# Blockwise VectorE transposes of x in the projections of a graph attention kernel

## The chip, the cores and the metric

The kernel runs on one core of one Trainium2 chip. The metric is the device time of one execution in microseconds (us): the median of several runs. A separate profiled execution gives the spans, waits and durations that this text quotes.

## What is computed

x has 3327 rows of 512 features in float32, adj is a 3327 x 3327 matrix of zeros and ones. A block of two attention layers is followed by a binarised linear layer. Cut to what matters:

```python
def gat_layer(x, W, adj):                 # twice, with W_stack[0] and W_stack[1]
    Wh, Ws = split(x @ W, 2, axis=-1)     # W is 512 x 1024
    a = softmax((Wh @ Ws.T), axis=-1) * adj
    return leaky_relu(a @ Wh + x, 0.01)

y = layernorm(x + gat_layer(gat_layer(x, W0, adj), W1, adj))
xw = maximum(sign(y), 0) @ sign(weight).T
out = layernorm(y + relu(adj @ xw))
```

## The kernel before

**Stages.** For each of the two layers l the kernel runs `project(l)` and then `attention(l)`; a last stage, `finale`, multiplies adj with the binarised layer's output. The change lies in `project`.

**Tiles.** A row tile is 128 rows of x (26 of them, t = 0 to 25; the last has 127 rows). A chunk c is four row tiles (7 chunks, 0 to 6; the last has two tiles). The 512 features are cut into four blocks k of 128 (`KD` = 4). TensorE contracts over partitions, so the projections need x with features on partitions: `xT[c]` is a tile of 128 partitions x 4 blocks k x 512 columns, a column being a row of x. There are two such buffers.

**From x to xT.** `load_x(c)` issues one DMA per row tile on SP (rows on partitions, 2 KB each; the last tile in two pieces of 112 and 15 rows). For layer 0 the source is x, for layer 1 it is x1_d, which attention of layer 0 writes. `transpose_x(c, k, lane)` makes one block k of xT: one TensorE transpose (L263) for each row tile of the chunk into a PSUM bank, and then one copy of 128x512 from PSUM into xT: by ScalarE (L268), or for chunk 0 by ScalarE and VectorE in turn (L121, L123 in `copy_out`). A chunk is so four such calls. For the last chunk GpSimd sets the one column without a row to zero (L273).

**W.** `load_x(0)`, the loads of W's left half into `wa` (L279) and right half (`load_w`, L207) and `load_x(1)` stand at the head of SP's queue in layer 0. W's rows are on partitions, in four blocks of 128 consecutive rows. The scores are computed as x M x^T with M = the Wh-half of W times the transposed Ws-half; `transpose_w` (L213) and `product_m` (L235) make M. For layer 1 this happens inside attention of layer 0.

**The projections.** Products are done by a seven-product scheme (Strassen-Winograd form): `seven` writes out the seven products with their copies and additions, `left_sums` (L180 to L183) and `right_sums` (L186 to L189) make the sums of operands on VectorE. For each pair of row tiles `keys(c, a)` makes the left sums of xT and stores xT and the sums to xs_d through GpSimd's queue (L325 to L327), and `project_values(c, a)` does the seven products with W (L338) and stores right sums of the result to ws_d. For each chunk `queries(c)` makes the right sums of xT (names xt) and does twice seven products with M and its sums msum (L394), and stores to gs_d.

**Order.** The main loop of `project` works on chunk c while it prepares chunk c + 1:

```python
turns = [lambda k=k: transpose_x(c + 1, k, tr_lane) for k in range(KD)]
pairs_of[c + 1] = project_values(c + 1, 0, acc_lane)
turns += [pairs_of[c + 1].pop(0), lambda: prepare(c + 1)]
```

`turns` are the four transposing steps, the left sums of the next chunk's first pair and the right sums of the next chunk. `weave` puts them in between the products of chunk c, evenly spread. x of chunk c + 2 is loaded at the start of the turn of chunk c. Each engine works off its own list in order and waits where an operand is not there yet. The row tiles, sums and many other tiles share a ring of buffers of 2 KB a partition (`slot`); a load waits until its buffer is free. In layer 1 the loads of the binarised layer's weights (L462) stand on SP among the loads of x, and their two operations per block (neg_w, L464, and bw, L466) among VectorE's work.

Of the kernel before, what the change touches and what calls it, by code (L numbers as in the profile page):

```python
# [9 lines left out]
F32 = mybir.dt.float32  # L10
# [9 lines left out]
P = 128  # L20
CT = 4
CW = CT * P
HW = CW // 2
NEG_SLOPE = 0.01
EPS = 1e-5
# [4 lines left out]
def kernel(  # L30
# [8 lines left out]
    nc = tc.nc  # L39
    N, D = x.shape  # L40
    L = w_stack.shape[0]
    KD = D // P
# [6 lines left out]
    def rows(t):  # L49
        return min(P, N - t * P)  # L50

    def tiles_of(c):
        return range(c * CT, min(NT, (c + 1) * CT))

    def halves_of(c):
        return [g for g in (2 * c, 2 * c + 1) if g < NQ]
# [5 lines left out]
    def half_cols(g):  # L62

        return g * HW, min(HW, N - g * HW)

# [11 lines left out]
    def slot(shape, dtype, name):  # L77
        return ring.tile(shape, dtype, tag="s", bufs=SBUFS, name=name)

    ident = keep.tile([P, P], F32, name="ident")  # L80
# [27 lines left out]
    ws_d = [tc.dram_tile([NQ, P, 4, HD], F32, name=f"ws_d{l}") for l in range(L)]  # L108
    gs_d = [tc.dram_tile([NC, P, 7, 2, HW], F32, name=f"gs_d{l}") for l in range(L)]

    def load_rows(eng, dst, src, r):

        cut = r - r % 16
        if cut:
            eng.dma_start(out=dst[:cut], in_=src[:cut])
        if cut < r:
            eng.dma_start(out=dst[cut:r], in_=src[cut:r])

    def copy_out(n, dst, src):
        if n % 2:  # L120
            nc.scalar.copy(dst, src)  # L121
        else:
            nc.vector.tensor_copy(dst, src)  # L123
# [20 lines left out]
    def seven(lane, name, multiply, c11, c12, c21, c22):  # L144
# [5 lines left out]
        def product(i, b, start):  # L150
            if start:
                bank[b] = pool.tile([P, HW], F32, tag=tag, name=f"p{b}_{name}")
            multiply(i, bank[b], start)

        def copied(i, b):
            if not held:
                two = slot([P, 2, HW], F32, f"h0_{name}"), slot([P, 2, HW], F32, f"h1_{name}")
                held.update(zip(("p1", "p5", "u2", "u3"), (t[:, e] for t in two for e in (0, 1))))
# [32 lines left out]
    def weave(*lists):  # L191

        at = [
            ((i + 0.5) / len(part), n, do)
            for n, part in enumerate(lists) for i, do in enumerate(part)
        ]
        for _, _, do in sorted(at, key=lambda e: e[:2]):
            do()

    ch_lane, acc_lane, tr_lane = (ps_ch, "ch"), (ps_acc, "acc"), (ps_tr, "tr")  # L200
    w_rows, wT, m_of, wsum_of = {}, {}, {}, {}

    def load_w(l, h):

        for k in range(KD):
            w_rows[l, h, k] = slot([P, D], F32, f"w{h}_{l}_{k}")
            nc.sync.dma_start(out=w_rows[l, h, k], in_=w_stack[l, ts(k, P), ts(h, D)])  # L207

    def transpose_w(l, h, k, lane):
        pool, tag = lane  # L210
# [32 lines left out]
    def project(l, pre):  # L243

        src = x if l == 0 else x1_d
        xTs, rows_of = {}, {}

        def load_x(c):
            rows_of[c] = []
            for t in tiles_of(c):  # L250
                xt = slot([P, D], F32, f"xr_{l}_{t}")
                load_rows(nc.sync, xt, src[t * P : t * P + rows(t), :], rows(t))
                rows_of[c].append(xt)

        def transpose_x(c, k, lane):
            if k == 0:
                xTs[c] = pre.tile([P, KD, CW], F32, tag="xT", bufs=2, name=f"xT_{l}_{c}")
            pool, tag = lane
            pt = pool.tile([P, CW], F32, tag=tag, name=f"pxt_{l}_{c}_{k}")
            w = 0  # L260
            for a, t in enumerate(tiles_of(c)):
                r = rows(t)
                nc.tensor.transpose(  # L263
                    pt[:, w : w + r], rows_of[c][a][:r, ts(k, P)], ident[:r, :r]
                )
                w += r
            if c:
                nc.scalar.copy(xTs[c][:, k, :w], pt[:, :w])  # L268
            else:
                copy_out(k, xTs[c][:, k, :w], pt[:, :w])  # L270
            n = len(tiles_of(c)) * P
            if w < n:
                nc.gpsimd.memset(xTs[c][:, k, w:n], 0.0)  # L273


        load_x(0)
        wa = pre.tile([P, KD, D], F32, tag="wa", bufs=1, name=f"wa_{l}")
        for k in range(KD):
            nc.sync.dma_start(out=wa[:, k], in_=w_stack[l, ts(k, P), :D])  # L279
        if l == 0:  # L280
            load_w(l, 1)
            for k in range(KD):
                w_rows[l, 0, k] = wa[:, k]
        load_x(1)
        for k in range(KD):
            transpose_x(0, k, acc_lane)
        if l == 0:
            for h in range(2):
                for k in range(KD):
# [5 lines left out]
        lo, hi = wa[:, 0:2], wa[:, 2:4]  # L295
# [34 lines left out]
        def project_values(c, a, lane):  # L330
            q = c * CT // 2 + a
            of = {}
            b12 = slot([P, HD], F32, f"wb12_{l}_{q}")
            b11, b21, b22 = (wh[q][:, i] for i in range(3))

            def multiply(i, bank, start):
                for k in range(2):
                    nc.tensor.matmul(  # L338
                        bank, of[LEFT[i]][:, k], wr[RIGHT[i]][:, k],
                        start=(start and k == 0), stop=(k == 1), skip_group_check=True,  # L340
                    )

            def done():
                t12 = slot([P, 2, HD], F32, f"t12_{l}_{q}")
                t34 = slot([P, 2, HD], F32, f"t34_{l}_{q}")
                right_sums(b11, b12, b21, b22, t12[:, 0], t12[:, 1], t34[:, 0], t34[:, 1])
                nc.gpsimd.dma_start(out=ws_d[l][q][:, 0:2], in_=t12)
                nc.gpsimd.dma_start(out=ws_d[l][q][:, 2:4], in_=t34)

            return (  # L350
                [lambda: of.update(keys(c, a))]
                + seven(lane, f"wh_{l}_{q}", multiply, b11, b12, b21, b22) + [done]
            )

        def queries(c, lanes):
# [3 lines left out]
            gs = {  # L359
                i: slot([P, 2, HW], F32, f"gsp_{l}_{c}_{i}")  # L360
                for i in (range(7) if len(halves_of(c)) == 2 else (B11, B21))
# [6 lines left out]
            if len(halves_of(c)) == 1:  # L368
                def one(e):
                    pg = ps_ch.tile([P, HW], F32, tag="ch", name=f"pg_{l}_{c}_{e}")  # L370
                    for k in range(KD):
                        nc.tensor.matmul(
                            pg, m[:, k, ts(e, P)], xT[:, k, :HW],
                            start=(k == 0), stop=(k == KD - 1),
                        )
                    copy_out(e, gs[B11 if e < 2 else B21][:, e % 2], pg)
# [44 lines left out]
        def prepare(c):  # L421
            start, *chains[c] = queries(c, (ch_lane, ch_lane if c else acc_lane))
            if start:
                start()
# [10 lines left out]
        for c in range(NC):  # L435
            turns = []
            if c + 1 < NC:
                turns = [lambda k=k: transpose_x(c + 1, k, tr_lane) for k in range(KD)]
                pairs_of[c + 1] = project_values(c + 1, 0, acc_lane)
                turns += [pairs_of[c + 1].pop(0), lambda: prepare(c + 1)]  # L440
            turns = rest + turns
            rest = [chains[c][1].pop()] if chains[c][1] else []
            if c + 2 < NC:
                load_x(c + 2)
            if c == 0:
                weave(*chains[c], turns)
            else:
                one, two = chains[c]
                pairs = pairs_of[c]
                for a in range(1, len(tiles_of(c)) // 2):  # L450
                    pairs += project_values(c, a, acc_lane)
                rest.append(pairs.pop())
                weave(one + two, pairs, turns)
# [15 lines left out]
    def attention(l, att):  # L469
# [116 lines left out]
        def column_max(c):  # L586
# [22 lines left out]
            def back():  # L609
                pb = ps_tr.tile([P, CW], F32, tag="tr", name=f"poff_{l}_{c}")  # L610
                for a in range(n):
                    nc.tensor.transpose(pb[:, ts(a, P)], rep[a], ident)
                for i, g in enumerate(halves_of(c)):
                    off[g] = att.tile([P, 1, HW], F32, tag=f"off{i}", bufs=1,
                                      name=f"off_{l}_{g}")
                    nc.vector.tensor_copy(off[g][:, 0], pb[:, ts(i, HW)])
# [336 lines left out]
    xw, xw_tiles, xt, ah, po = {}, [], {}, {}, {}  # L953
# [51 lines left out]
    def finale(att):  # L1005
# [78 lines left out]
        for g in range(NQ):  # L1084
# [30 lines left out]
            for _, do in sorted(work, key=lambda e: e[0]):  # L1115
                do()
        inexact = nc.values_load(flag_i[0:1, 0:1], min_val=0, max_val=2 * CW)
        with tc.If(inexact < 1) as cmp:
# [70 lines left out]
```

## Time and profile before

| | us |
|---|---|
| median of 3 runs | 2652.82 (2652.31 to 2653.39) |
| the profiled execution: its time | 2652.55 |
| the profiled execution: its span | 2650.7 |
| ScalarE copies of xT (L268), 48 | 26.5 busy |
| TensorE waiting for VectorE or ScalarE in the projection of layer 1 | 1.4 |
| TensorE waiting for the first loads of x in layer 0 | 5.6 |

The span is the time from the first to the last instruction of the profiled execution; 1.85 us lie around it. "Busy" is the time in which an engine had an instruction running; matmuls overlap one another, so that the distance between the starts of two of them and not their duration tells what one costs. PE is TensorE, PEld its loads of the stationary operand, DVE VectorE, ACT ScalarE, POOL GpSimd, and SP issues most of the loads. The projection of layer 0 takes the first 190 us or so, that of layer 1 lies between about 1257 and 1430 us. The chain of waits that ended last consists of TensorE's matmuls of the final product and, at the very end, of the additions and the normalisation of the last rows.

### The profile page before, as it was taken

To read this page: it belongs to the slowest core of one execution; us is meant where nothing else is said; L and a number is where in the kernel's file an instruction comes from. 1 tells how busy PE (TensorE), PEld (TensorE's weight loads), DVE (VectorE), ACT (ScalarE), POOL (GpSimd) and SP (SyncE) were. 2 spreads that over 40 slices of the span, in tenths; PEclk is the share of its full clock that TensorE was granted. 3 is DMA by queue.
4 is the path that set the end of the run, shared out by engine and by line. 5 is a ranking of instruction groups with operands and counts; after the bars stand their busy time and mean duration, and the time that the engine had idled before them with its cause. 6 is when DMAs were issued, how large, how long until landed. Compare 5 with 4: busy or idle time off the path is not lost. (4 is left out here: it accounts for less than half of the span.)

```text
span 2650.7 us, 40451 instructions
## 1 busy us (share of the span) xinstructions
PE 2614.6 (99%) x12839; PEld 2271.0 (86%) x12864; DVE 2046.3 (77%) x4211; ACT 812.1 (31%) x2000; POOL 1091.3 (41%) x2029
## 2 busy tenths in 40 slices
PE   9999999999999999999999999999999999999998
PEld 7888888888888888887888888888888888888787
DVE  5554888899888896666754589988899888767976
ACT  3333332333333332221333333333333333222143
POOL 2550343444444444546552044444444444455510
PEclk9999999999999999999999999999999999999999
DMA  5754777777777776776865677777777777677875
GB/s 205 272 193 157 260 239 251 253 266 252 259 244 244 267 248 222 235 245 230 294 219 180 210 231 272 241 257 260 233 270 247 252 255 236 228 260 260 278 245 168
DMA packets 285186, 638.63 MB, mean 241 GB/s; under 512 B 32141, under 2 KB 146671, under 8 KB 283430
## 3 DMA queue, kind: packets, MB, share of 16 engines
q1 hardware_dynamic: 249206, 529.52, 60.4%
q0 software_dynamic: 35760, 106.45, 10.8%
q8 instruction: 105, 1.72, 0.3%
q14 instruction: 115, 0.94, 0.1%
HBM read 528.91 MB, written 106.93 MB: 240 GB/s over the span
## 5 line engine op out<-in xcount | busy, mean ns | idle before, releaser
L500 PE MATMUL pZ<-gs,xs 128*128 128x256 f32 x2496 | 636.2, 379 | 1.7 <-ACT u L517 1.7
L699 POOL TENSOR_TENSOR as<-s 128x128 f32<-128x128 f32 x338 | 163.4, 484 | 1037.0 <-DVE s L661 691.9
L500 PEld LDWEIGHTS pZ<-gs,xs 128*128 128x128 f32 x2496 | 473.3, 190 | 67.8 <-ACT u L517 3.6
L726 PE MATMUL acc<-ws,s 128*128 128x256 f32 x1352 | 402.6, 379 | 0.0
L726 PE MATMUL acc<-wh,s 128*128 128x256 f32 x1352 | 355.9, 379 | 0.0
L726 PE MATMUL acc<-ws,as 128*128 128x256 f32 x1352 | 349.7, 380 | 1.8 <-POOL as L701 1.2
L648 ACT ACTIVATE s<-s 128x512 f32<-128x512 f32 x338 | 213.3, 631 | 377.7 <-DVE s L645 377.1
L500 PE MATMUL pY<-gs,xs 128*128 128x256 f32 x1248 | 320.7, 379 | 2.2 <-ACT p L517 2.2
L726 PEld LDWEIGHTS acc<-ws,as 128*128 128x128 f32 x1352 | 255.2, 190 | 42.3 <-issue 5.8
L726 PEld LDWEIGHTS acc<-wh,s 128*128 128x128 f32 x1352 | 257.3, 190 | 35.2
L726 PEld LDWEIGHTS acc<-ws,s 128*128 128x128 f32 x1352 | 256.2, 190 | 34.4
L570 DVE TENSOR_TENSOR top<-top,s 128x512 f32<-128x512 f32 x312 | 225.4, 735 | 69.0 <-ACT s L557 48.5
L500 PEld LDWEIGHTS pY<-gs,xs 128*128 128x128 f32 x1248 | 236.7, 190 | 36.0 <-ACT p L517 3.8
L645 DVE TENSOR_TENSOR s<-s,off 128x512 f32<-128x512 f32 x338 | 249.2, 737 | 0.1
L661 DVE TENSOR_TENSOR s<-s,adj 128x512 f32<-128x512 f32 x338 | 236.8, 701 | 9.4 <-DMA adj<-in_adjT_dram 1.0
L656 DVE TENSOR_TENSOR total<-total,s 128x512 f32<-128x512 f32 x312 | 231.8, 743 | 0.0
L517 ACT COPY u<-pZ 128x256 f32<-128x256 f32 x312 | 115.8, 371 | 345.5 <-PE pZ L500 344.9
L701 POOL TENSOR_TENSOR as<-s 128x128 f32<-128x128 f32 x338 | 204.7, 606 | 26.5
L726 PE MATMUL acc<-wh,as 128*128 128x256 f32 x676 | 203.0, 382 | 0.0
L700 POOL TENSOR_TENSOR s<-s 128x128 f32<-128x128 f32 x338 | 183.3, 542 | 27.6
L702 POOL TENSOR_TENSOR as<-s,as 128x128 f32<-128x128 f32 x338 | 180.7, 535 | 26.5
L542 DVE TENSOR_TENSOR s<-p,u 128x256 f32<-128x256 f32 x156 | 66.8, 428 | 151.7 <-ACT u L517 151.7
(206 smaller groups left out, 3883.9 us busy)
## 6 DMA issues: line engine op xcount, KB each, us to landing
ws<-ws_d SPq DMA_DIRECT2D x338, 512.0 KB, 3.8
xs<-xs_d SPq DMA_DIRECT2D x182, 512.0 KB, 5.8
adj<-in_adjT_dram SPq DMA_DIRECT2D x324, 256.0 KB, 4.2
xs<-xs_d SPq DMA_DIRECT2D x156, 384.0 KB, 6.5
gs_d<-gsp POOLq DMA_DIRECT2D x88, 256.0 KB, 2.8
gs<-gs_d SPq DMA_DIRECT2D x12, 1792.0 KB, 10.9
adj_d<-ab POOLq DMA_DIRECT2D x169, 112.0 KB, 3.8
ahl<-adj_d SPq DMA_DIRECT2D x78, 224.0 KB, 4.7
```

What stands on the lines that cost most here:

```text
L500: nc.tensor.matmul(ch[bank], xs[c, q, a][:, k], gs[c][:, b, k], start=(start and k == 0), stop=(k == 1), skip_group_check=True,)
L517: nc.scalar.copy(ch[name], ch[bank])
L570: nc.vector.tensor_tensor(top[i], top[i], t, ALU.max)
L645: nc.vector.tensor_tensor(s, s, off[g].to_broadcast([P, 2, HW]), ALU.subtract)
L648: nc.scalar.activation(sc[g, q], sc[g, q], AF.Exp)
L656: nc.vector.tensor_tensor(total[g], total[g], sc[g, q], ALU.add)
L661: nc.vector.tensor_tensor(s, s, adj[g, q], ALU.mult)
L699: nc.gpsimd.tensor_tensor(s3, a11, a21, ALU.subtract)
L700: nc.gpsimd.tensor_tensor(a21, a21, a22, ALU.add)
L701: nc.gpsimd.tensor_tensor(s2, a21, a11, ALU.subtract)
L702: nc.gpsimd.tensor_tensor(s4, a12, s2, ALU.subtract)
L726: nc.tensor.matmul(acc[g][i // 2][:, i % 2], a[i], b[i], start=(q == 0 and i % 2 == 0), stop=(q == NQ - 1), skip_group_check=True,)
```

## The change

In every chunk but the first of each layer x is transposed by VectorE, one instruction for a row tile. That instruction transposes within blocks of 32 partitions by 32 columns. So that the blocks end where they belong, the tile is loaded differently: the rows of the tile are split into four groups r of 32, the features into four groups a of 128, and feature group a of row 32 r + v goes to partition 32 a + v, columns 128 r to 128 r + 127. One tile is four DMAs, one for each a, with runs of 512 bytes. After the transpose partition 32 a + u holds the features 128 a + 4 u + k for block k: partition p of block k is feature 4 p + k, every fourth feature. The read of the transpose steps by four elements (16 bytes), its writes are runs of 32.

The same assignment of features is used everywhere in `project`: `w_rows_of` takes rows 4 p + k of W for block k, and `transpose_first`, which keeps chunk 0 on TensorE, reads every fourth column of the row tile as stationary operand. In the last tile GpSimd clears the last row group before the load, which comes in twelve pieces.

```diff
+    def load_laid(eng, dst, src, n):
+
+        full = n // B
+        cut = (n - full * B) // 16 * 16
+        for a in range(P // B):
+            if full:
+                eng.dma_start(
+                    out=dst[ts(a, B), :full],
+                    in_=src[: full * B, ts(a, P)].rearrange("(r v) f -> v r f", v=B),
+                )
+            for lo, hi in ((0, cut), (cut, n - full * B)):
+                if lo < hi:
+                    eng.dma_start(
+                        out=dst[a * B + lo : a * B + hi, full],
+                        in_=src[full * B + lo : full * B + hi, ts(a, P)],
+                    )
+
+    def w_rows_of(l, h, k):
+
+        return w_stack[l, :, ts(h, D)].rearrange("(p k) n -> k p n", k=KD)[k]
...
-            nc.sync.dma_start(out=w_rows[l, h, k], in_=w_stack[l, ts(k, P), ts(h, D)])
+            nc.sync.dma_start(out=w_rows[l, h, k], in_=w_rows_of(l, h, k))
...
-                xt = slot([P, D], F32, f"xr_{l}_{t}")
-                load_rows(nc.sync, xt, src[t * P : t * P + rows(t), :], rows(t))
+                some = src[t * P : t * P + rows(t), :]
+                if c == 0:
+                    xt = slot([P, D], F32, f"xr_{l}_{t}")
+                    load_rows(nc.sync, xt, some, rows(t))
+                else:
+                    xt = slot([P, P // B, P], F32, f"xr_{l}_{t}")
+                    if rows(t) < P:
+                        nc.gpsimd.memset(xt[:, rows(t) // B :], 0.0)
+                    load_laid(nc.sync, xt, some, rows(t))
...
+        def transpose_first(k, lane):
...
+            for a in range(CT):
+                xt = rows_of[0][a].rearrange("r (p k) -> r k p", k=KD)
+                nc.tensor.transpose(pt[:, ts(a, P)], xt[:, k], ident)
+            copy_out(k, xTs[0][:, k], pt)
+
+        def transpose_x(c, a):
+            if a == 0:
                 xTs[c] = pre.tile([P, KD, CW], F32, tag="xT", bufs=2, name=f"xT_{l}_{c}")
-            pool, tag = lane
-            pt = pool.tile([P, CW], F32, tag=tag, name=f"pxt_{l}_{c}_{k}")
-            w = 0
-            for a, t in enumerate(tiles_of(c)):
-                r = rows(t)
-                nc.tensor.transpose(
-                    pt[:, w : w + r], rows_of[c][a][:r, ts(k, P)], ident[:r, :r]
-                )
-                w += r
-            if c:
-                nc.scalar.copy(xTs[c][:, k, :w], pt[:, :w])
-            else:
-                copy_out(k, xTs[c][:, k, :w], pt[:, :w])
-            n = len(tiles_of(c)) * P
-            if w < n:
-                nc.gpsimd.memset(xTs[c][:, k, w:n], 0.0)
+            nc.vector.transpose(
+                xTs[c][:, :, ts(a, P)].rearrange("p k (r v) -> p r k v", v=B),
+                rows_of[c][a].rearrange("p r (u k) -> p r k u", u=B),
+            )
...
-            nc.sync.dma_start(out=wa[:, k], in_=w_stack[l, ts(k, P), :D])
+            nc.sync.dma_start(out=wa[:, k], in_=w_rows_of(l, 0, k))
...
-                turns = [lambda k=k: transpose_x(c + 1, k, tr_lane) for k in range(KD)]
+                turns = [
+                    lambda a=a: transpose_x(c + 1, a) for a in range(len(tiles_of(c + 1)))
+                ]
```

Built, the changed kernel keeps the order of the other instructions on TensorE, ScalarE and VectorE but for one place: on VectorE, at the start of layer 1, the eight operations on the binary weights (L464, L466) stand differently among the sums. `turns` still has six steps (four in the turn before the last chunk), and the calls for one chunk are now the row tiles and not the blocks k.

More of the change, by code (lines that the diff above doesn't have):

```diff
@@ L22 @@
 CW = CT * P
+B = 32
 HW = CW // 2
@@ L250, in load_x @@
             for t in tiles_of(c):
-                xt = slot([P, D], F32, f"xr_{l}_{t}")
-                load_rows(nc.sync, xt, src[t * P : t * P + rows(t), :], rows(t))
+                some = src[t * P : t * P + rows(t), :]
[7 more added lines that the diff above has]
+                    load_laid(nc.sync, xt, some, rows(t))
                 rows_of[c].append(xt)
-        def transpose_x(c, k, lane):
+        def transpose_first(k, lane):
             if k == 0:
-                xTs[c] = pre.tile([P, KD, CW], F32, tag="xT", bufs=2, name=f"xT_{l}_{c}")
-            pool, tag = lane
-            pt = pool.tile([P, CW], F32, tag=tag, name=f"pxt_{l}_{c}_{k}")
-            w = 0
-            for a, t in enumerate(tiles_of(c)):
-                r = rows(t)
-                nc.tensor.transpose(
-                    pt[:, w : w + r], rows_of[c][a][:r, ts(k, P)], ident[:r, :r]
-                )
-                w += r
-            if c:
-                nc.scalar.copy(xTs[c][:, k, :w], pt[:, :w])
-            else:
-                copy_out(k, xTs[c][:, k, :w], pt[:, :w])
-            n = len(tiles_of(c)) * P
-            if w < n:
-                nc.gpsimd.memset(xTs[c][:, k, w:n], 0.0)
+                xTs[0] = pre.tile([P, KD, CW], F32, tag="xT", bufs=2, name=f"xT_{l}_0")
+            pool, tag = lane
+            pt = pool.tile([P, CW], F32, tag=tag, name=f"pxt_{l}_{k}")
+            for a in range(CT):
[4 more added lines that the diff above has]
+            if a == 0:
+                xTs[c] = pre.tile([P, KD, CW], F32, tag="xT", bufs=2, name=f"xT_{l}_{c}")
+            nc.vector.transpose(
+                xTs[c][:, :, ts(a, P)].rearrange("p k (r v) -> p r k v", v=B),
+                rows_of[c][a].rearrange("p r (u k) -> p r k u", u=B),
+            )
         load_x(0)
@@ L285, in project @@
         for k in range(KD):
-            transpose_x(0, k, acc_lane)
+            transpose_first(k, acc_lane)
         if l == 0:
```

## The prediction

> **What bounds the kernel now.** I read the busy table of the page first, then the waits of TensorE over the whole span, then the windows of the two projection stages, where the whole change lies, and last the timelines there.
>
> ```profile
> PE 2614.6 (99%) x12839; PEld 2271.0 (86%) x12864; DVE 2046.3 (77%) x4211; ACT 812.1 (31%) x2000; POOL 1091.3 (41%) x2029
> ...
> L263 PE MATMUL pxt<-ident,xr 128*128 128x128 f32 x208 | 33.4, 285 | 5.7 <-DMA xr<-in_x_dram 5.6
> ```
> The reader sees TensorE at 99%, and the 208 transposes of x: 4 per row tile, 26 tiles, 2 layers. Their 285 ns each are no price, because matmuls overlap. The price is the distance between starts:
>
> ```profile
> 63.66 0.60 PE L263 MATMUL pxt<-ident,xr 128*128 128x128 f32 x4
> ...
> 64.10 1.03 PE L394 MATMUL pY_g<-xT,msum 128*128 128x256 f32 x4
> ...
> 64.97 1.03 PE L338 MATMUL pZ_wh<-wsum,xT 128*128 128x256 f32 x4
> ```
> In this timeline (start, duration) four transposes take 64.10 - 63.66 = 0.44 us of TensorE, 0.11 us each. A product of four matmuls takes about 0.86 us. No line shows a gap: transposes stand in a closed queue and fill no hole.
>
> ```profile
> 53.70:79.60 25.90, 25.90 (x129) 22.81 (x129) 14.93 (x34) 9.79 (x24) 12.80 (x22) 1.00 0.88 324
> 79.60:105.50 25.90, 25.90 (x130) 22.81 (x129) 15.68 (x37) 9.79 (x24) 14.37 (x24) 1.00 0.82 293
> ...
> 1256.90:1287.10 30.20, 28.77 (x147) 24.56 (x146) 25.62 (x61) 12.48 (x27) 15.68 (x25) 1.00 0.68 225
> ```
> In these windows (stretch, length, then PE, PEld, DVE, ACT, POOL busy, clock, DMA share, GB/s) one chunk of x costs 25.9 us with TensorE full and VectorE at 15.7 us. The start of layer 1 differs: VectorE is busy for 25.6 of 30.2 us, and TensorE loses 1.4 us.
>
> ```profile
> 1276.42 0.60 PE L263 MATMUL pxt<-ident,xr 128*128 128x128 f32 x4
> ...
> 1277.45 1.99 PE L394 MATMUL pZ_g<-xt,msum 128*128 128x256 f32 x8 [0.43 <-DVE xt L187]
> ```
> Here TensorE waits for a sum that VectorE makes late. This is the place to watch.
>
> **What the Trainium skill says.** "VectorE: DVE Perf Modes", section on the three transpose paths, gives 311 ns for a VectorE transpose of 128x128 and says that it works in 32x32 blocks. The trace has none. It does show VectorE's pace: a two-input operation takes 683 ns for 128x512 and 417 ns for 128x256, so 1.04 ns an element. "TensorE: Matmul & The Clock Gate", section on LDWEIGHTS, prices a weight load at columns / 1.2 ns, 107 ns for 128; the trace agrees, since transposes follow each other every 0.11 us. "SBUF — State Buffer", in the note on cachelines in its section on the DMA port swizzle, says that SBUF is read in lines of 16 bytes and that a read which goes to a new line each time pays a penalty, of no stated size. Both new reads step by 16 bytes; nothing in the trace steps so. "DMA: Bandwidth & Descriptors", Specifications, puts the smallest transfer at line rate at 512 B. The stores of xT into xs_d move 512-byte runs and land 128 KB in 3.4 us, which does not contradict it.
>
> **The change part by part.**
>
> Removed from TensorE: the transposes of chunks 1 to 6. Per layer these are 5 chunks x 16 + 8 = 88, so 176 of 208. At 0.11 us: 176 x 0.11 = 19.4 us. None of it lay under a wait of TensorE in the steady chunks, so all of it counts there.
>
> Removed from ScalarE: 48 copies out of PSUM (26.5 us in all). ScalarE is at 38% there and TensorE waits on it for 0.6 us in both projections together; I count nothing.
>
> Added to VectorE: 44 transposes of 128x512, one per row tile. The skill's 311 ns less 128 x 1.04 leaves 178 ns fixed, so 178 + 512 x 1.04 = 0.71 us as an estimate; a plain copy of this size (0.55 us) is the floor, and twice the element time (1.2 us) is what I take as the dear end if the 16-byte step hurts. I take 0.71. A steady chunk then has 15.7 + 4 x 0.71 = 18.5 us of VectorE under 25.9 - 4 x 0.44 = 24.2 us of TensorE: covered, 76%. In the burst at a chunk's end (VectorE without a break from 78.47 to 85.74) the sums for the next chunk are ready some 4 us ahead of their product, and the built order puts the transposes before that burst, one at a time between additions that wait for TensorE anyhow. So: nothing in the eight steady chunks. If the cover goes, it costs 4 x the excess per chunk.
>
> Start of layer 0: four transposes stand close together behind the sums of m. VectorE there idles 5.5 us before 50.02 and the products have 3 us in hand: nothing.
>
> Start of layer 1: here VectorE has no idle time. The order of the built kernel moves the two binary-weight operations per row block (L464, L466) to before the sums xt of chunk 0, all four pairs now. Before, the first stood before three sums of m and held them for a load (2.83 us). I lay the new order out with the durations of the trace: sums of m to 1267.8, two additions to 1268.6, then binary weights with one load in between to about 1275, and the sum that TensorE waits for ends near 1277.3, as before. TensorE arrives 2 x 0.44 = 0.88 us earlier and waits so much longer: +0.9 us of the gain is given back. Then VectorE does the rest of these sums and eight more (to 1281.9), four transposes and four additions (to 1286.4); the next chunk's first product can come at 1286.1 and needs the transposes, done at 1285.6. That is a margin of 0.5 us. I count 0.5 us for the roughness; beyond 0.83 us a transpose each further 0.1 us costs 0.4.
>
> First chunks: still 16 transposes on TensorE per layer, whose stationary operand now steps by 16 bytes. If a weight load takes twice as long, 32 x 0.107 = 3.4 us; nothing if the step is free. I take the middle, 1.7 us.
>
> Loads of x: a tile comes in 4 pieces of 64 KB in 512-byte runs, so 16 issues on SP instead of 4 per chunk, at 0.33 us or so each, 5 us. Behind them on SP: at the start of layer 1 the four loads of the binary weights, which wait until 1264.9 for a buffer anyway; then chunks 2 and 3. Chunk 2 was issued from 1273.7 and its transposes come at about 1291. With 16 issues at 0.5 us and 5 us to landing it is there by 1287. Elsewhere a chunk is loaded over 20 us ahead, even where a load took 13.4 us to land. Nothing, at worst a few us at this one place, because a VectorE that waits for a tile holds the additions behind it.
>
> The last tile: one 0.3 us memset on GpSimd per layer, before its twelve small loads, in place of 8 column memsets; SP waits for it with nothing urgent behind. W's row loads keep count and size. Nothing.
>
> Sum: -19.4 + 0.9 + 0.5 + 1.7 = -16.3 us. The profiled execution took 2652.55 (span 2650.7 and 1.85 around it), giving 2636.2; the median is 0.27 higher, so 2636.5.
>
> **The rivals.**
>
> Half-speed transposes: the step costs VectorE a cycle more per element, T = 1.2 us. A chunk is still covered (20.5 under 24.2), but layer 1's start loses 4 x 0.5 - 0.5 = 1.5 us more, and weight loads with the same step pay their full 3.4. Sum -16.3 + 1.5 + 1.7 = -13.1: 2640. For it: the note on lines; against it: no number.
>
> A late tile: the loads of chunk 2 in layer 1 slip behind 16 issues and DMA engines that are 80% busy there, VectorE waits in order, TensorE behind it. About 5 us: 2641. Against it: 4 us of margin.
>
> Slower: VectorE becomes the bound of the projections. A chunk takes 15.7 + 4T; it passes the old 25.9 at T = 2.55 us. Counting 8 full chunks and both starts, loss and gain meet at T = 2.34. At T = 3 us: 8 x 1.8 = +14.2, half chunks -1.8, the starts +6.9 and +4.4, weight loads +1.7: +25, 2678. For it: strided reads with unstated penalty, one operation that the trace never shows; against it: it needs over four times the pace of every other VectorE operation here.
>
> That the change removes nothing because transposes filled holes is excluded by the timeline.
>
> **How the numbers follow.** Forecast 0.60 (2636.5), half speed 0.20 (2640), late tile 0.08 (2641), slower 0.06 (2678), and 0.06 for a transpose of 2.2 to 2.5 us, which ends within 0.2%. The range: at the low end nothing is paid for weight loads and roughness and a little of layer 1's wait goes (-20.5 and rounded, 2631); at the high end half speed and a late tile partly add (2644). A measurement here tells 0.2%, 5.3 us, from no change. So faster 0.88, same 0.06, slower 0.06.
>
> **What would show it.** TensorE: 32 transposes left, no gaps in the steady windows, a chunk every 24.2 us instead of 25.9. VectorE: transposes of about 0.7 us and near 18.5 us busy a chunk. The wait before the first product with a sum in layer 1 grows to 1.3 us or so. The transposes of the first chunks 0.11 us apart (step free) or 0.21 (doubled). A chunk time above 24.5, or waits of TensorE for VectorE in the steady windows, would make the prediction wrong; so would a VectorE transpose above 1.3 us.

## The result and the profile after

| | before | after |
|---|---|---|
| median, us (4 runs each, taken together) | 2653.11 (2652.31 to 2653.85) | 2637.01 (2634.56 to 2638.11) |
| ratio to before, 95% interval | | 0.9938 [0.9921, 0.9955] |
| profiled execution, us | 2652.55 | 2636.88 |
| its span, us | 2650.7 | 2635.0 |

The change makes the kernel faster by 0.6%. The profiled execution is 15.67 us shorter; the sum of the prediction was 16.3. The end agrees; several of its terms do not, as the rest of this text shows.

The busy table of the page of the changed kernel:

```profile
PE 2596.6 (99%) x12688; PEld 2254.8 (86%) x12688; DVE 2086.2 (79%) x4255; ACT 786.8 (30%) x1952; POOL 1089.2 (41%) x2023
```

VectorE gained 44 instructions and 40 us, ScalarE lost 48 and 25 us, and TensorE lost 18 us of busy time. The two kinds of transposes, from the groups of the changed kernel (busy time, mean ns of one, idle time of the engine before them):

```profile
L301 DVE STREAM_TRANSPOSE xT<-xr 128x512 f32<-128x512 f32 x44 | 47.9, 1098 | 0.0
...
L295 PE MATMUL pxt<-ident,xr 128*128 128x128 f32 x32 | 6.6, 359 | 5.4 <-DMA xr<-in_x_dram 5.4
```

Of TensorE's 208 transposes 32 are left. VectorE's take 1.10 us each, not the 0.71 of the prediction. That this costs nothing in the steady chunks is seen in the windows of the changed kernel, one chunk of x each (stretch, length, then PE, PEld, DVE, ACT, POOL busy, granted clock, DMA share, GB/s):

```profile
53.20:77.40 24.20, 24.20 (x114) 21.32 (x113) 18.70 (x38) 7.44 (x20) 11.84 (x20) 1.00 0.86 310
...
101.50:125.70 24.20, 24.20 (x113) 21.30 (x113) 19.26 (x41) 7.44 (x20) 14.05 (x24) 1.00 0.64 221
```

A chunk takes 24.20 us instead of 25.90, with TensorE full and VectorE at 19.3. Between 40 and 190 us no line of the waits has TensorE waiting.

The start of layer 1 is another matter. TensorE there in the changed kernel (start, duration; in brackets the idle time just before and what ended it):

```profile
1249.34 2.10 PE L295 MATMUL pxt<-ident,xr 128*128 128x128 f32 x16
...
1264.92 1.89 PE L425 MATMUL pZ_g<-xT,m 128*128 128x256 f32 x8
1268.56 1.99 PE L425 MATMUL pX_g<-xT,m 128*128 128x256 f32 x8 [1.75 <-DVE wb L187]
1271.68 1.97 PE L425 MATMUL pZ_g<-xt,msum 128*128 128x256 f32 x8 [1.13 <-DVE xt L212]
...
1280.39 1.03 PE L369 MATMUL pZ_wh<-wa,xT 128*128 128x256 f32 x4
```

It waits twice, 2.88 us together, where before it waited 0.43. (Two earlier waits of 0.60 and 0.36 us are the same in both kernels.) In starts the cost is larger, because a group of eight matmuls takes 1.73 us from start to start when nothing is missing: 3.37 us are lost from 1264.92 to 1273.48, against 0.69 before. The first wait is for wb, an addition on VectorE, and VectorE's own timeline of the same stretch says why that addition is late:

```profile
1266.68 0.43 DVE L497 TENSOR_SCALAR neg_w<-wT 128x512 bf16<-128x512 f32 x1 [3.07 <-DMA wT<-in_weightT_dram]
1267.14 0.69 DVE L499 SCALAR_TENSOR_TENSOR bw<-wT,neg_w 128x512 bf16<-128x512 f32 x1
1267.76 0.42 DVE L187 TENSOR_TENSOR wh<-h_wh,h_wh 128x256 f32<-128x256 f32 x1
1268.09 0.41 DVE L187 TENSOR_TENSOR wb<-pY_wh,h_wh 128x256 f32<-128x256 f32 x1
...
1277.24 3.08 DVE L301 STREAM_TRANSPOSE xT<-xr 128x512 f32<-128x512 f32 x3
```

VectorE stands idle for 3.07 us before the third neg_w, whose weights have not landed, and the additions of the products are queued behind it. The four transposes of the next chunk end at 1280.32, and TensorE's first product of that chunk starts at 1280.39 without a wait.

The start of layer 0 has a third difference. TensorE before, and then after:

```profile
9.93 2.39 PE L213 MATMUL pwT<-ident,wa 128*128 128x128 f32 x16
12.15 2.08 PE L213 MATMUL pwT<-ident,w 128*128 128x128 f32 x16
14.06 1.02 PE L235 MATMUL pm<-wTs,wTs 128*128 128x512 f32 x2
```

```profile
9.67 3.18 PE L238 MATMUL pwT<-ident,wa 128*128 128x128 f32 x16
12.68 0.49 PE L238 MATMUL pwT<-ident,w 128*128 128x128 f32 x3
13.35 1.20 PE L238 MATMUL pwT<-ident,w 128*128 128x128 f32 x9 [0.17 <-DMA w<-in_w_stack_dram]
14.79 0.66 PE L238 MATMUL pwT<-ident,w 128*128 128x128 f32 x4 [0.24 <-ACT wTs L146]
15.28 1.02 PE L260 MATMUL pm<-wTs,wTs 128*128 128x512 f32 x2
```

The transposes of W's right half now break off for a load, and the first product of M (pm) starts 1.22 us later. (In both kernels the early transposes stand 0.21 us apart and the later ones 0.11; e9 below shows that this is not what makes pm late.)

**Where the time went.** Four starts on TensorE cut the span: the first product of M (pm); the first score product of layer 0's attention; the first transpose of layer 1; the first score product of layer 1's attention. All of the profiles below, in us:

| kernel | pm starts at | projection 0 | attention 0 | projection 1 | the rest | span |
|---|---|---|---|---|---|---|
| before | 14.06 | 181.40 | 1061.49 | 171.85 | 1221.90 | 2650.7 |
| after | 15.28 | 171.73 | 1062.33 | 164.86 | 1220.80 | 2635.0 |
| e1, unit step | 15.42 | 171.73 | 1061.52 | 165.14 | 1220.69 | 2634.5 |
| e2, features only | 14.05 | 182.07 | 1060.85 | 172.87 | 1221.06 | 2650.9 |
| e3, TensorE's put back | 15.34 | 181.39 | 1061.22 | 174.58 | 1220.17 | 2652.7 |
| e4, binary weights late | 15.71 | 171.73 | 1060.62 | 161.47 | 1223.87 | 2633.4 |
| e5, twice | 16.24 | 175.17 | 1064.34 | 173.57 | 1221.48 | 2650.8 |
| e6, thrice | 15.45 | 193.32 | 1061.77 | 193.21 | 1222.45 | 2686.2 |
| e7, one load a tile | 13.75 | 171.73 | 1061.35 | 164.14 | 1221.43 | 2632.4 |
| e8, binary weights spread | 14.84 | 171.72 | 1063.39 | 161.49 | 1220.76 | 2632.2 |
| e9, pieces later too | 14.27 | 171.73 | 1061.98 | 161.48 | 1220.64 | 2630.1 |
| e10, after again | 15.31 | 171.73 | 1064.94 | 166.34 | 1220.98 | 2639.3 |

Of these columns, projection 0 repeats to 0.01 us in seven profiles that have nothing late there; attention 0, where these kernels differ in little but W's order of rows, ranges over 4 us. (In e5 and e10, the two longest there, TensorE's granted clock was at half for 3.4 us of it.) So the parts can be read far more finely than the total. Each row is one execution; that of e5 is the slowest of its 13, 4 us above their median. From before to after: start +1.22, projection 0 -9.67, projection 1 -6.99, attention and rest -0.26: -15.70.

### The profile page after: what moved, and what is told of

Read it like the earlier page. It is cut to its first block, busy times and chain, and to the rows that moved or that the text cites. A ratio compares the mean times of both kernels' runs of the same rounds, so it can differ in the third digit from the quotient of the medians.

```text
span 2635.0 us, 40312 instructions
## 1 busy us (share of the span) xinstructions
PE 2596.6 (99%) x12688; PEld 2254.8 (86%) x12688; DVE 2086.2 (79%) x4255; ACT 786.8 (30%) x1952; POOL 1089.2 (41%) x2023
```

## The experiments

The theory after the result: the gain is TensorE's 176 transposes and nothing else; VectorE's slower transposes are covered; the losses are the late loads at the two starts. The rivals: part of the gain is in ScalarE's copies or in the new order of work; the 16-byte step costs time on TensorE; VectorE is nearly the bound.

**e1: the step of VectorE's reads.**

```diff
-                rows_of[c][a].rearrange("p r (u k) -> p r k u", u=B),
+                rows_of[c][a].rearrange("p r (k u) -> p r k u", u=B),
```

> The changed kernel, but the VectorE transposes read 32 neighbouring columns instead of every fourth (block k then holds features 128a + 32k + u, which no longer match W's rows; everything else is as in the changed kernel). Theory A, the 16-byte step is what makes a transpose last 1.10 us: its duration falls to about 0.71 us, and the two waits of TensorE at the start of layer 1 (1.7 and 1.1 us) shrink little, since the binary weights stand ahead of them and only later work follows the transposes; time 2636 to 2637 us. Rival B, a transpose of 4-byte elements runs at half of VectorE's pace whatever it reads: the duration stays at 1.10 us and the time at 2637.

This version leaves W's rows as they are, so that features and rows no longer match. Measured: 2639.65 us (2636.31 to 2642.42), ratio 0.9953 [0.9938, 0.9968]. That is above the forecast, but the interval overlaps that of after. The transposes in the groups of e1:

```profile
L301 DVE STREAM_TRANSPOSE xT<-xr 128x512 f32<-128x512 f32 x44 | 30.5, 700 | 0.0
```

0.70 us with neighbouring elements, 1.10 with the step: the step costs 0.40 us or 57%, and 44 times that, 17 us of VectorE, moves neither projection by more than 0.3 us. The Trainium skill, "SBUF — State Buffer", in the note on cachelines in its section on the DMA port swizzle, names a penalty for reads that go to a new 16-byte line each time, without a size. The measurement fits that; here it is 0.40 us per 512 elements. The estimate of 0.71 us from "VectorE: DVE Perf Modes", The three transpose paths, came out right for a float32 read of neighbouring elements, though the page's 311 ns is for bf16; the form in the kernel is another.

**e2: the features alone.** The kernel before, with W's rows 4p + k and with every fourth column as stationary operand in all 208 transposes:

```diff
-                    pt[:, w : w + r], rows_of[c][a][:r, ts(k, P)], ident[:r, :r]
+                    pt[:, w : w + r], rows_of[c][a].rearrange("r (p k) -> r k p", k=KD)[:r, k],
+                    ident[:r, :r]
```

> The kernel before with only the assignment of features changed (rows 4p + k of W in block k, every fourth column of x as stationary operand of all 208 TensorE transposes); x is loaded, copied and cleared as before, VectorE transposes nothing. Theory A, the step of 16 bytes is almost free for a weight load (16 transposes of layer 1's first chunk took 1.95 us in the changed kernel): groups of four transposes 0.44 to 0.50 us apart, time 2653 to 2656 us. Rival B, a stepped weight load takes twice as long: groups 0.86 us apart, time near 2672. The first product of M in layer 0 starts at 15.3 us if the rows 4p + k of W (or the stepped first chunk) cause the late start of the changed kernel there, at 14.1 us if they do not.

Measured: 2654.5 us (2652.57 to 2657.68, 20 runs), ratio 1.0006 [0.9999, 1.0012]. TensorE's timeline in a steady chunk of e2:

```profile
63.81 0.63 PE L267 MATMUL pxt<-ident,xr 128*128 128x128 f32 x4
64.28 1.03 PE L399 MATMUL pY_g<-xT,msum 128*128 128x256 f32 x4
```

Four transposes take 0.47 us and not 0.44, and the projections grow by 0.7 and 1.0 us over 104 transposes each, so the step costs TensorE under 0.01 us a weight load. The weight load itself does get longer (median 207 ns instead of 141), but the starts do not move apart with it: the load runs beside the matmul ahead of it. The first product of M starts at 14.05 us, so W's new order of rows has no part in the late start.

**e3: TensorE's transposes put back** beside VectorE's, into PSUM that nobody reads:

```diff
+        def again(c, k):
+            pt = ps_tr.tile([P, CW], F32, tag="tr", name=f"pxt_{l}_{c}_{k}")
+            for a, _ in enumerate(tiles_of(c)):
+                nc.tensor.transpose(pt[:, ts(a, P)], rows_of[c][a][:, k], ident)
...
-                    lambda a=a: transpose_x(c + 1, a) for a in range(len(tiles_of(c + 1)))
+                    lambda k=k, n=n: (again(c + 1, k), k < n and transpose_x(c + 1, k))
+                    for k in range(KD)
```

> The changed kernel with the 176 TensorE transposes put back beside the VectorE transposes, at the places where the kernel before has them, into PSUM banks that nobody reads and nobody copies. Theory A, the gain is TensorE's time alone, at 0.11 us a transpose: +19.4 us, near 2656. Rival B, a good part of the gain came from the copies that ScalarE no longer makes and the PSUM bank that TensorE no longer waits for: clearly less than +19 us comes back, say 2645 to 2650.

Measured: 2655.58 us (2653.86 to 2659.39), ratio 1.0011 [1.0002, 1.002], 18.6 us above after. The window of one chunk of e3:

```profile
53.20:79.10 25.90, 25.90 (x130) 22.81 (x129) 19.08 (x40) 7.45 (x20) 12.72 (x21) 1.00 0.83 300
```

The chunk is back at 25.90 us while ScalarE's copies stay away (7.45 us) and VectorE keeps its transposes (19.08). Projection 0 is 181.39, as before, and projection 1 is 9.72 us longer than in after: 19.4 us together for 176 transposes. So the gain is TensorE's time, all of it; freeing ScalarE gave nothing.

**e4: the binary weights out of layer 1's projection**, to the start of layer 1's attention, in one place:

```diff
-        if last:
-            binary_weights()
-        else:
+        if not last:
...
+            if last and v == 8 - LOOK:
+                binary_weights()
```

> The changed kernel with the loads and the eight VectorE operations of the binary weights moved from the start of layer 1's projection into the beginning of its attention stage, where VectorE is half idle. Theory A, these eight operations and the loads that they wait for, not the VectorE transposes, cause the waits of 1.7 and 1.1 us: both waits fall below 0.3 us in total, time about 2634 us (-2.5 to -3). Rival B, VectorE is overfull there with the 4.4 us of transposes: TensorE waits as long at the first product of chunk 1 instead, time 2637.

Measured: 2635.2 us (2634.43 to 2637.94), ratio 0.9936 [0.9922, 0.9949]: no faster than after that can be told. The landmarks split this into two. Projection 1 is 3.39 us shorter, both waits gone; that is what they cost in starts (3.37). The rest is 3.07 us longer, and the waits of e4 in that stage have a new line (engine, tile and line, what it waited for: us in total, times, longest):

```profile
PE pZ L533 <- DMA xs<-xs_d: 2.2, 1, 2.2
```

On SP the weights' third load waited for a buffer (it went out 6.8 us after the second), and the loads of the attention's operands stood behind it. That is 2.2 of the 3.07 us; the remainder is not traced. The cause of the two waits is shown; the place was badly chosen.

**e8: the binary weights one block at a time**, four steps of the attention apart, each loaded two steps ahead of its operations:

```diff
+    def binary_load(k):
+        wt = w_of[k] = ring.tile([P, D], F32, tag="h", name=f"wT_{k}")
+        nc.sync.dma_start(out=wt, in_=weightT[ts(k, P), :])
...
+            if last:
+                for k in range(KD):
+                    if u == 4 + 4 * k:
+                        binary_load(k)
+                    if u == 6 + 4 * k:
+                        binary_weights(k)
```

> The changed kernel with the binary weights moved into the beginning of layer 1's attention as in the fourth run, but one block at a time, four steps apart, each load two steps ahead of its operations, so that SP never waits for a buffer there. Theory A, the fourth run gave back 2.2 us only because SP stood behind the third block's load: layer 1's projection again takes about 161.5 us and the rest 1220.8, span near 2631, time 2632 to 2633. Rival B, VectorE or the DMA engines have no room there either: 2635 as in the fourth run.

Measured: 2632.93 us (2630.74 to 2634.01), ratio 0.9919 [0.9902, 0.9935]. Projection 1 is 161.49 and the rest 1220.76: the 3.4 us are gained and not given back.

**e5 and e6: how much VectorE may cost.** Each transpose is done twice (2.2 us a tile) or three times (3.3 us):

```diff
-            nc.vector.transpose(
...
+            for _ in range(2):
+                nc.vector.transpose(
...
```

> The changed kernel with every VectorE transpose done twice into the same place, 2.2 us a row tile. Theory A, the sum of the prediction holds: VectorE then has 15.7 + 8.8 = 24.5 us in a chunk of 24.2, and the starts of both layers lose up to 4.4 and 1 us; by the prediction's sum (40 x T - 93.7 against the kernel before) 2647 us, some +10 on the changed kernel. Rival B, in-order queues make VectorE bind well before it is full: 2655 or more. Rival C, there is more cover than the sum says: 2637 to 2641.

> The same with every VectorE transpose done three times, 3.3 us a row tile: the slower rival of the prediction. Theory A: VectorE binds, a chunk takes 15.7 + 13.2 = 28.9 us, and the time is 40 x 3.3 - 93.7 = +38 us on the kernel before, near 2691. Rival B, other waits soften it: below 2675.

Measured: e5 2648.58 us (2646.3 to 2652.65), ratio 0.998 [0.9972, 0.9989]; e6 2688.02 us in its one run. A window of e6, and its waits of TensorE in projection 0:

```profile
60.00:89.00 29.00, 25.11 (x103) 21.15 (x104) 28.52 (x50) 6.71 (x18) 14.84 (x25) 0.90 0.86 305
```

```profile
PE pZ_wh L370 <- DVE s L206: 10.8, 5, 2.7
PE pX_g L426 <- DVE b L187: 6.2, 4, 4.9
```

At three transposes VectorE is busy for 28.52 of 29 us and TensorE waits for its sums and additions: the rival in which VectorE is the bound, made real. (The granted clock of 0.90 in this window adds its part.) The kernel before took 2653.74 us beside these two; e5 is 5.2 us below it and e6 34.3 above. On a straight line between them, loss and gain meet at a transpose of 2.3 us, an estimate from two points, one of them a single run. The kernel's 1.10 us is less than half of that.

**e7: one load a tile.** One DMA of 2 KB runs, as before, in place of the four pieces:

```diff
-                    load_laid(nc.sync, xt, some, rows(t))
...
+                    load_rows(
+                        nc.sync, xt.rearrange("p r f -> p (r f)"), some, rows(t)
+                    )
```

> The changed kernel, but a row tile comes with one DMA in runs of 2 KB as in the kernel before (the rows then lie on partitions as they come, so that the VectorE transposes put them in wrong places; the instructions and their times are the same). Theory A, the late start of layer 0's first product of M (15.3 us instead of 14.1) comes from the 16 small loads of chunk 1 behind W's loads: it goes back to about 14.1 and the total falls by 1 us or so, 2635 to 2636. Rival B, the start depends on something else (the clock's rise or the stepped weight loads): it stays near 15.3 and the total at 2637.

This version leaves the rows where they are loaded, so that the blocks come out in wrong places. Measured: 2634.27 us (2633.8 to 2634.77), ratio 0.9926 [0.991, 0.9943], 2.7 us below after, with intervals that overlap. TensorE at the start of e7:

```profile
11.77 2.14 PE L238 MATMUL pwT<-ident,w 128*128 128x128 f32 x16
13.75 1.02 PE L260 MATMUL pm<-wTs,wTs 128*128 128x512 f32 x2
```

The sixteen transposes of W's right half run through, and pm starts 1.53 us earlier than in after. In projection 1 the landmark falls by 0.72 us. SP's queue shows what the pieces cost there; first after, then e7:

```profile
1241.42 9.24 SPq L129 DMA_DIRECT2D xr<-x_d  x16
1257.30 6.33 SPq L495 DMA_DIRECT2D wT<-in_weightT_dram  x4
```

```profile
1239.10 3.17 SPq L116 DMA_DIRECT2D xr<-x_d  x4
...
1254.78 8.99 SPq L497 DMA_DIRECT2D wT<-in_weightT_dram  x4
```

Sixteen issues hold SP for 9.24 us, four for 3.17. Yet the first weight load starts 7.96 us after the first transpose of layer 1 (1249.34) in after and 7.95 us after it in e7 (1246.83), so it waited for a buffer and not for SP. What differs is VectorE's order, and so e7 changes more than its edit says. VectorE in e7:

```profile
1264.00 0.42 DVE L187 TENSOR_TENSOR wb<-pY_wh,h_wh 128x256 f32<-128x256 f32 x1
1265.12 0.43 DVE L499 TENSOR_SCALAR neg_w<-wT 128x512 bf16<-128x512 f32 x1 [0.69 <-DMA wT<-in_weightT_dram]
```

The first wb stands ahead of the third neg_w here, as in the kernel before, and not behind it, as in after. TensorE's waits at this place are 0.18, 1.36 and 0.35 us instead of 1.75 and 1.13, although the third weight load lands later than in after, counted from layer 1's first transpose (18.3 us against 17.3). The versions without pieces (before, e2, e7) all have this order, and those with pieces and with the weights in this place (after, e1, e3, e5, e6, e10) all have the other. So the pieces bring the other order, and the 0.72 us goes with it. Why the build orders the work so is not shown.

**e9: the pieces of chunk 1 after W.** e8, and in layer 0 the pieces are issued by GpSimd once the first products run:

```diff
-        load_x(1)
+        if l > 0:
+            load_x(1)
...
-            weave(product_m(l, acc_lane), first + second, [lambda: prepare(0)])
+            weave(
+                product_m(l, acc_lane), first + second,
+                [lambda: load_x(1, nc.gpsimd), lambda: prepare(0)],
+            )
```

> Version e8 (binary weights one block at a time), and in layer 0 the pieces of x for chunk 1 are issued on GpSimd's queue once the first products run, and not on SP straight behind W's loads. Theory C (the 512-byte pieces, moved at the same time as W's right half, make W land late): TensorE's 16 transposes of w run without a wait, the first product of M starts at 14.1 us or before (before 14.06, one load per tile 13.75, after 15.28, e8 14.84), and the time falls by 0.7 to 1.2 us on e8, to about 2632. Rival (the first loads just vary from run to run, or SP's issue and not the transfers is what is late): the first product of M stays at 14.8 to 15.4 and the time at e8's. The rest of the landmarks stays as in e8: layer 0's projection 171.7 us from there, layer 1's 161.5.

Measured: 2632.8 us (2631.99 to 2636.12), ratio 0.9926 [0.9909, 0.9942]. TensorE at the start of e9:

```profile
12.39 2.04 PE L238 MATMUL pwT<-ident,w 128*128 128x128 f32 x16
14.27 1.02 PE L260 MATMUL pm<-wTs,wTs 128*128 128x512 f32 x2
```

The wait is gone. The time from issue to landing of the four loads of W's right half, first in after, then in e9:

```profile
DMA to landing us min/median/max: 6.0/6.2/6.5
```

```profile
DMA to landing us min/median/max: 5.4/5.8/6.0
```

Four profiles without the pieces beside W (before, e2, e7, e9) have the slowest of these loads at 5.8 to 6.1 us and pm at 13.75 to 14.27; eight with them (after, e1, e3, e4, e5, e6, e8, e10) have it at 6.3 to 7.6 us and pm at 14.84 to 16.24. The medians overlap (5.9 in before and in e3). The last of the four loads lands at 12.10 to 12.41 us of the span without the pieces and at 12.86 to 14.26 with them, and in all eight pm starts 1.97 or 1.98 us after that landing. So the rival of chance falls, and so does that of the clock's rise, which e7's expectation named: transposes stand 0.11 us apart from 10.44 us on in e10 and from 12.71 on in e1, and pm starts at 15.31 and 15.42. SP's issue is not it either, since the last of W's loads goes out at 6.8 us in after and in e9.

In e9 pm is 0.17 later than the theory allowed. There the landing no longer sets it; the transposes ahead stand 0.21 us apart until 11.55. The median did not follow the landmark: the forecast fall of 0.7 to 1.2 us on e8 is below what runs of one kernel differ by.

**e10: after again**, one more profile:

> The changed kernel once more, profiled a second time, for how far its landmarks repeat. If the late start is the pieces' doing the first product of M starts at 15.0 or later again (15.28 the first time); if it is chance it can fall anywhere from 13.8 on. Waits of TensorE in layer 1's projection again 1.7 and 1.1 us, within 0.3 each, and layer 1 takes 164.9 from its first transpose to the first score product, within 0.3; if the order of the binary weights against their loads sets them, they repeat, and if a late transfer does they move.

Measured: 2641.09 us, one run. The late start repeats (15.31). The waits of layer 1 do not repeat as forecast. TensorE there in e10:

```profile
1267.56 1.89 PE L425 MATMUL pZ_g<-xT,m 128*128 128x256 f32 x8
1272.29 2.77 PE L425 MATMUL pX_g<-xT,m 128*128 128x256 f32 x8 [2.84 <-DVE wb L187]
1274.86 2.90 PE L425 MATMUL pZ_g<-xt,msum 128*128 128x256 f32 x8
1277.59 1.89 PE L425 MATMUL pY_g<-xt,msum 128*128 128x256 f32 x8
```

The sum of the waits is the same, 2.84 us instead of 1.75 + 1.13, but it comes in one piece, because the first two weight loads landed later here (VectorE waits 1.35 us for the first instead of 0.19). After it the next two groups take 2.57 and 2.73 us from start to start where the following one takes 1.73: TensorE's granted clock fell. Three windows of e10 show it (the third column from the right is the clock):

```profile
1269.95:1273.36 3.41, 1.07 (x5) 0.97 (x6) 2.91 (x7) 0.00 (x0) 0.00 (x0) 1.00 0.51 143
1273.36:1276.77 3.41, 3.41 (x10) 2.40 (x9) 3.38 (x8) 0.00 (x0) 0.00 (x0) 0.50 0.46 132
1276.77:1280.18 3.41, 3.41 (x17) 3.00 (x16) 3.38 (x9) 1.49 (x4) 2.21 (x5) 1.00 0.72 235
```

So projection 1 takes 166.34 us and not 164.86, with the same wait. When the weights land differs from run to run, and with it what this order costs.

## Why the prediction was right

The forecast of 2636.5 us and 2637.01 measured agree to 0.02%. By its terms:

- **-19.4 us, TensorE's transposes.** Held. Layer 0: 88 x 0.11 = 9.68, measured 9.67. Layer 1 shows the same once its waits are taken off (6.99 and 2.68 make 9.67), and e3 gives 18.6 us back.
- **ScalarE's copies, nothing.** Held: in e3 they are gone and no time goes with them.
- **A VectorE transpose of 0.71 us.** Mis-sized: 1.10. The half-speed rival had the duration nearly right (1.2), but neither of the costs that it drew from it came. The steady chunks were covered as forecast (VectorE at 19.3 of 24.2 us, forecast 18.5). At layer 1's start the text let each 0.1 us beyond 0.83 cost 0.4 us, which would be 1.1 us; e1 against after shows none (165.14 and 164.86). The timeline gives the likely reason: TensorE had already waited, and the transposes end 0.07 us ahead of its product.
- **+1.7 us for stepped weight loads.** Mis-sized: about nothing. The 16 transposes that open layer 1 take 1.95 us from their first start to the next product, before (1256.95 to 1258.90) and after (1249.34 to 1251.29); e2 bounds the cost at 0.01 us each. The load did lengthen, from 141 to 207 ns, but the starts did not follow: its length is not the price that the term took it for.
- **+0.9 and +0.5 us at layer 1's start.** The mechanism was right, a TensorE that arrives 0.88 us earlier and waits longer, and the size was not: its waits on VectorE grow by 2.45 us (2.88 less 0.43), which costs 2.68 us in starts (3.37 less 0.69) where the two terms allow 1.4. The wait that was forecast, before the first product with a sum, came nearly as said (1.13 us, forecast 1.3); the one of 1.75 us a product earlier was not seen. The working laid the weights' operations out "with one load in between"; VectorE in fact waited 3.7 us for those loads, 3.07 of it in front of an addition that TensorE needed. e4 and e8 take the operations away and shorten this projection by 3.4 us.
- **Loads of x, nothing.** Wrong. The text watched chunk 2 of layer 1, where nothing came late, and not the transfers that run beside the pieces: W's right half at the start of layer 0 lands too late, +1.22 us in the profile. Nor did it see that the pieces bring the new order of VectorE's work, which it took as given. Without the pieces e7 gains 1.53 us at the one place and 0.72 at the other. The sixteen issues themselves took 9.24 us and not 5; no wait of TensorE is traced to that.
- **The sum.** 1.7 too much for the weight loads stood against 1.28 and 1.22 too little for the two starts. That the total is right to 0.02% is luck in so far as these offset one another; the term of 19.4 us is what makes it right within a few us.
- **The slower rival.** Its point of no gain, 2.34 us a transpose, agrees with the 2.3 that e5 and e6 give.

The best versions that were run are e8 and e9: 2632.9 and 2632.8 us, some 0.8% below before and 4 us below the change. The intervals of their ratios overlap that of after; that e8 is better rests on the 3.4 us in projection 1, which e4, e8 and e9 show alike.

## What to carry to other kernels

Work on a full TensorE was worth its start-to-start distance times its count. Moving it to an engine that was still a quarter free afterwards was safe here even though the new operation takes half as long again as thought: work out the duration at which that engine becomes the bound, and see how far it is. An operation that waits for a load must not stand in front of additions that the critical engine needs; place it where its engine has slack, one at a time, and look at which loads stand behind its load in the issuing queue. When a load is cut into pieces, ask which other transfers run at that moment and whether the order of other engines' work changes, not only whether the pieces come in time.

## What the hardware showed unexpectedly

- A 16-byte step in the reads costs VectorE's transpose 0.40 us in 0.70, and TensorE's stationary operand next to nothing in time, though its load grows from 141 to 207 ns.
- Pieces of 64 KB in runs of 512 bytes made other loads beside them land later (W's right half: the slowest load took 6.3 to 7.6 us in eight profiles with them and 5.8 to 6.1 in four without). "DMA: Bandwidth & Descriptors", Specifications, counts 512 B as enough for line rate; no run here measures the rate of the pieces by itself, only that their neighbours are later.
- One wait of 2.84 us lowered TensorE's granted clock in e10 (to 0.50 for 3.41 us), and that cost 1.5 us on top; the same wait in two parts in after left it at 1.00, and so did one of 2.85 us in e5. "TensorE: Matmul & The Clock Gate", Part 1, describes a free-running window of about 3.4 us in which the engine's activity is judged, and has the clock fall after at least one idle window. The traces agree with the window: in all twelve profiles every stretch between two changes of the granted clock is a whole multiple of 3.413 us, counted from its first rise. They differ on the idle time, and the measurement decides: the clock falls 31 times, each time after a window in which TensorE was idle for 2.01 us or more, and never after one with 1.94 us or less (the ends of matmuls are modelled, so these limits are rough). In e10 the wait left 2.34 of 3.41 us of one window idle; in after the waits left 1.55 and 1.33 us in two windows, and the one in e5 left 1.88 and 1.42. So what a wait costs depends on where it lies against this window.
